# Two banded gated layers on one core: the same instructions in another order within a pipeline step

## Chip, cores and metric

One NeuronCore of a Trainium2 chip runs the whole program. The metric is device time in microseconds (us), from one launch. The engines are TensorE (PE), ScalarE (ACT), VectorE (DVE), GpSimd (POOL) and SyncE (SP), which here only issues DMAs. Each runs its own instruction list in order and waits on semaphores for the others.

## What is computed

The input `x` is one image of 512x512 positions with 64 channels, in float32. Two layers of the same form, with weights of their own, follow each other:

```python
def layer(x):                       # x = x + layer(x), twice
    xn    = ln(group_norm(x)) * norm_scale + norm_bias     # over the 64 channels
    left  = (xn @ Wl + bl) * mask * sigmoid(xn @ Wlg + blg)    # 64 -> 128
    right = (xn @ Wr + br) * mask * sigmoid(xn @ Wrg + brg)
    gate  = sigmoid(xn @ Wog + bog)
    out   = banded(left, right, 4)  # out[i, j] = sum over |d| <= 4 of left[i+d, i] * right[i+d, j]
    out   = (ln(out) * out_norm_scale + out_norm_bias) * gate  # over the 128 channels
    return out @ Wo + bo            # 128 -> 64
```

The band multiplies rows of `right` by a narrow band of `left`, for each of the 128 channels on its own.

## The kernel before

**Tiling.** Rows go in 9 blocks of 64 (a block and its halo). A block is cut into 2 chunks of columns, so a layer has 18 chunks, and a chunk has 16 steps. A step `t` takes one unit: 8 columns of the left half of the image and the same 8 of the right half, 64 rows each, which fill 128 partitions. Layer 1 has 288 steps and a lead-in and run-out, and layer 2 the same. In this text r is `t` modulo 16.

**One loop over steps, written out by hand.** `layer()` is a Python loop over `t`. In each step it calls the helper functions in a fixed order, and `en.*` (class `InOrder`, whose line 373 therefore stands for nearly all instructions in the profile) keeps that order on every engine. Nothing is rescheduled afterwards. So the order of the calls is the order in which each engine, and SP's DMA queue, works. A step works on several units at once, at different stages of a software pipeline:

- `load`, `fetch`, `take_left`, `recall` (SP): DMAs of the unit some steps ahead, of the residual tile `XR` (4 buffers) for step t+1, of band tiles `A`, and of the transposed unit `zg` for step t+2.
- `affine` (POOL, 2 instructions) and `inner_norm` of the unit of step t+2 (POOL, 2 instructions): first normalization, on tile `z`. `inner_stats` (DVE, 4 `BATCH_NORM_STATS2` on `sti`).
- `transposed` of the unit of step t+1 (PE transposes into PSUM), then `kept` (ACT writes `zT`, SP stores it).
- `right` of the unit of step t, in two halves (q = 0 and q = 4): `projected` (PE, from `zT`), a sigmoid (ACT, `sg`), a product (DVE, `RO`).
- `gates` (PE from `zg`, then two ACT sigmoids into `gate`), `turned` (PE transposes of `on`, then two DVE products into `ZH`), `biased` (POOL, adds the bias to `XR`), `end` of step t-1 (PE, from `ZH`; one DVE addition into `XR`; two stores on SP), `sums` of step t-2 (PE, in layer 1 alone), `norm` for step t+1 (ACT, 8 instructions `on<-RO,nm,rs`).
- `mix` (the band, in place on `RO`): 32 matmuls on PE, then one half of the result copied by ACT and one by DVE. DVE's copy waits for ACT's copy of the same band group.
- `out_stats` (DVE, `sto<-RO`), 3 to 7 in a step, called `looking`. `solve`, in steps with r = 0, 4, 8 and 12: five small DVE instructions (`var`, `nm`, `rs`), then twelve small POOL instructions (`rsqrt`, `rs`, `nm`), which give the scales that `inner_norm` (from step t+1 on) and `norm` (called in step t+1) need.

Band groups are not spread evenly, and neither are the POOL affines:

```python
step = [t0 + n for n, k in enumerate((2, 1, 2, 2, 1, 2, 1, 2, 2, 1)) for _ in range(k)]
count = [1, 1, 2, 1, 2, 1, 1, 2, 1, 1, 1, 0, 1, 1, 0, 0]
```

So steps with r = 0, 2, 3, 5, 7, 8 have two band groups, those with r = 1, 4, 6, 9 one, and r = 10 to 15 none. `count` is the number of units that are affined on POOL in a step with that r; in steps with r = 0, 4, 8, 12 the next step's are done as well.

**Buffers that couple the engines.** PSUM pool `ps2` has two buffers, which the right halves, `transposed` and the band groups take in turn. Pool `ps` (3 buffers in layer 1, 4 in layer 2) is taken in turn by the two `gates`, the two `turned` and the `end` of a step. `on` and `gate` have one buffer, `sg` and `zT` two, `ZH` two pairs.

**Short names.** For PE's groups in a step: P0 and P4 are the two halves of the right projection, G the gate matmuls, T the transposes of `turned`, X those of `transposed`, E the matmuls of `end`, S those of `sums`, B one band group. PE's order before is P0, G, P4, T, X, E, S, B, B. ACT's is sigmoid of P0, two gate sigmoids, sigmoid of P4, `zT`, 8 of `norm`, copies. DVE's is up to three `out_stats`, product of P0, up to two `out_stats`, product of P4, the two `ZH` products, other `out_stats`, `inner_stats`, addition of `end`, `solve`, copies.

Of the kernel before, what the change touches and what calls it, by code (L numbers as in the profile page):

```python
# [79 lines left out]
def tile_two_banded_layers(  # L80
# [301 lines left out]
    class Unit:  # L382
# [3 lines left out]

        def __init__(self, at: int, blk: Block = None, j: int = 0, near: int = None):
            self.at, self.blk, self.j, self.near = at, blk, j, near

    def load(src: bass.AP, u: Unit):  # L390
        u.z = zp.tile([P, JU, D], F32, tag="z", name="z")
# [93 lines left out]
        return pr  # L485

    def right(u: Unit, q: int, w: dict):
        pr = projected(u, q, w["right"]).rearrange("p e k h -> p (e k) h")
        sg = wk.tile([P, JQ, H], F32, tag="sg", name="sg", bufs=2)
        en.scalar.activation(sg, pr[:, :, H:], AF.Sigmoid)  # L490
        en.vector.tensor_tensor(
            RO[:, :, u.c + q : u.c + q + JQ, :],
            pr[:, :, :H].rearrange("p j (h t) -> p h j t", t=2),
            sg.rearrange("p j (h t) -> p h j t", t=2), ALU.mult,
        )

    def left(u: Unit, q: int, w: dict):
# [38 lines left out]
            )  # L536
        return A

    def mix(c: int, A: bass.AP, h0: int):


        j0 = c % 2 * (JC - JW)
        R = RO[:, :, j0 : j0 + JC, :]
        pb = two_banks()
        ph = pb.rearrange("i (h j) -> i h j", j=JC)
        for turn in range(2):
            for h in range(HB // 2):
                for e in range(2):
                    part = slice(e * S, (e + 1) * S)
                    hh = (turn ^ e) * (HB // 2) + h  # L550
                    en.tensor.matmul(
                        ph[part, hh, :], lhsT=A[part, :, h0 % HA + hh],
                        rhs=R[part, (h0 + hh) // 2, :, hh % 2],
                        start=True, stop=True,
                    )
        q = HB // 4
        for n in range(2):
            o = R[:, h0 // 2 + n * q : h0 // 2 + (n + 1) * q]
            v = pb.rearrange("i (h t j) -> i h j t", t=2, j=JC)[:, n * q : (n + 1) * q]
            if n == 0:  # L560
                en.scalar.copy(o, v)
            else:
                en.vector.tensor_copy(o, v)

    class Out:

# [40 lines left out]
            for n, o in enumerate(outs):  # L607
                o.rs, o.nm = ro[:, n * JU : (n + 1) * JU], nm[:, n * JU : (n + 1) * JU]

    def norm(o: Out):  # L610
        o.on = onp.tile([P, JU, H], F32, tag="on", name="on")
        for j in range(JU):
            en.scalar.activation(
                o.on[:, j, :].rearrange("p (h t) -> p h t", t=2), RO[:, :, o.c + j, :],
                AF.Identity, bias=o.nm[:, j : j + 1], scale=o.rs[:, j : j + 1],
            )
# [5 lines left out]
    def gates(o: Out, w: dict):  # L622
        b = o.blk
        n = 2 * JQ * b.m
        pgs = [one_bank()[:, :n].rearrange("h (k p) -> h k p", p=b.m) for e in range(2)]
        for e, pg in enumerate(pgs):
            part = slice(e * D, (e + 1) * D)
            en.tensor.matmul(
                pg, lhsT=w["gate"][part],
                rhs=o.t[part].rearrange("c k (e p) -> c (k e) p", e=2)[:, :, b.lo : b.hi],  # L630
                start=True, stop=True,
            )
        g = gp.tile([H, 4 * JQ * (S - WIN)], F32, tag="gate", name="gate")
        for e, pg in enumerate(pgs):
            en.scalar.activation(
                g[:, e * n : (e + 1) * n].rearrange("h (k p) -> h k p", p=b.m), pg, AF.Sigmoid
            )

        o.g = g[:, : 2 * n].rearrange("h (x n p) -> h n x p", n=2, p=b.m)

    def turned(o: Out, w: dict):

        b = o.blk
        pts = [one_bank().rearrange("h (x p) -> h x p", p=S) for n in range(2)]
        for e in range(2):
            for k in range(JQ):
                for n, pt in enumerate(pts):
                    part = slice(n * S, (n + 1) * S)
                    en.tensor.transpose(
                        pt[:, e * JQ + k, :], o.on[part, place(k, e), :], ident[part, part]  # L650
                    )
        for n, pt in enumerate(pts):
            en.vector.scalar_tensor_tensor(
                ZH[(2 * o.n + n) % len(ZH)][:, :, : b.m], pt[:, :, b.lo : b.hi], w["ob"],
                o.g[:, n], ALU.add, ALU.mult,
            )
# [13 lines left out]
        add = fewer if stats and o.blk.m < S - WIN else w["add"]  # L670
        en.gpsimd.tensor_tensor(f, f, mid(add[:n], JU // 2), ALU.add)

    def end(dst: bass.AP, o: Out, w: dict):
        m = o.blk.m
        po = one_bank().rearrange("i (j c) -> i j c", c=D)
        for k in range(JQ):
            for e in range(2):
                for n in range(2):

                    en.tensor.matmul(  # L680
                        po[n * S : (n + 1) * S, 2 * k + e, :],
                        lhsT=ZH[(2 * o.n + n) % len(ZH)][:, e * JQ + k, :], rhs=w["Wo"],
                        start=True, stop=True,
                    )
        f = o.xr[: S + m, :, 1 : 1 + 2 * D]
        en.vector.tensor_tensor(
            f, po[: S + m].rearrange("i (k t) c -> i k (t c)", t=2), f, ALU.add
# [16 lines left out]
    def layer(src: bass.AP, dst: bass.AP, w: dict, stats: bool, then=None):  # L704
# [60 lines left out]
        for t in range(min(loads), last_t + 3):  # L765
# [19 lines left out]
                n = (len(os) - 1) * (JU // 2)  # L785
                looking.append((o, st[:, n : n + JU // 2, :], k))

            for v in looking[:3]:
                out_stats(*v)

            for u in affines.pop(t, []):
                affine(u, en.vector if u.at < NU + 4 else en.gpsimd)
            if t % 4 == 0 and t > NU:
                then_affine = affines.pop(t + 1, [])

            todo = []
            for at, u in inners.get(t, []):
                key = (at + 1) // 4
# [5 lines left out]
                todo += [(u, st[:, n : n + JU // 2, :], k) for k in range(JU // 2)]  # L804
                us.append(u)

            if t in units:
                right(units[t], 0, w)
            for v in looking[3:5]:
                out_stats(*v)  # L810
            if t in outs:
                gates(outs[t], w)
            if t in units:
                right(units[t], JQ, w)
            if t in lefts:
                for q in range(0, min(JU, NEAR * JQ - lefts[t].near), JQ):
                    left(lefts[t], q, w)
            for u in inputs(t + 2):
                inner_norm(u)
            if t in outs:  # L820
                turned(outs[t], w)
            for u in inputs(t + 1):
                transposed(u)
                kept(u)
            if t in outs:
                biased(outs[t], w, stats)
            for v in looking[5:]:
                out_stats(*v)
            for v in todo:
                inner_stats(*v)  # L830
            if t - 1 in outs:
                end(dst, outs[t - 1], w)
            if stats and t - 2 in outs:
                sums(outs[t - 2], t - 2 == first_t, t - 2 == last_t)
            if t % 4 == 0:
                st, us = sti.pop((t + 4) // 4, (None, []))
                so, os = sto or (None, [])
                sto = None
                for u in then_affine:
                    affine(u, en.gpsimd)  # L840
                then_affine = []
                if us or os:
                    solve(w, us, os, st, so)
            if t + 1 in outs:
                norm(outs[t + 1])
            for n, (c, h0) in enumerate(mixes.get(t, [])):
                mix(c, A[c, h0 // HA], h0)

    class Slices:

# [131 lines left out]
```

## Time and profile before

| what | value |
|---|---|
| timed runs | 4960.42, 4958.66, 4958.12 us; median 4958.66 |
| span of the profiled execution | 4957.7 us (its time is not listed apart; the median is 0.96 us above the span) |
| busy share of the span | PE 84%, PE weight loads 71%, DVE 77%, ACT 74%, POOL 77% |
| mean granted TensorE clock | 0.940 |
| first group statistics, before layer 1 | about 300 us, DVE and DMA |
| layer 1, its steps with full work | about 541 to 2436 us from the span's start |
| run-out of layer 1 and lead-in of layer 2 | about 2436 to 2900 us |
| layer 2, its steps with full work | about 2900 to 4680 us |

A line of the profile's groups reads: source line, engine, operation, output tile <- input tiles, shape, xcount, busy time. A timeline line has the start in us from the span's start, the duration, the engine and the group, and in brackets the idle time before it with what ended it. Instructions overlap on an engine, so the pitch (start to start) is shorter than the duration. An idle time that ends with a semaphore from another engine is put down to that engine.

### The profile page before, as it was taken

The page shows a single profiled execution, that of the slowest core. Times are in us where ns is not written, and L with a number is a line of the kernel's source. Part 1 is how long each engine was busy: PE and PEld are TensorE (multiplying, and loading weights), DVE is VectorE, ACT ScalarE, POOL GpSimd, SP SyncE. Part 2 cuts the span into 40 slices and gives each one's busy share as a digit, 9 for nine tenths or more (in the row PEclk, how much of TensorE's full clock was granted, in tenths as well). Part 3 has the DMA queues.
Part 4 walks back from the last instruction along what each step waited for, and adds up shares of the span by engine and source line. Part 5 has one row for each costly group of instructions (what it writes and reads, how often), then busy time and mean ns, then how long its engine had stood idle before and what let it go on. Part 6 is the DMA issues. An engine that isn't in the chain of part 4 may idle for free. (4 is left out here: it accounts for less than half of the span.)

```text
span 4957.7 us, 173298 instructions
## 1 busy us (share of the span) xinstructions
PE 4186.4 (84%) x67090; PEld 3543.6 (71%) x67090; DVE 3836.3 (77%) x9635; ACT 3645.2 (74%) x8156; POOL 3826.5 (77%) x4739
## 2 busy tenths in 40 slices
PE   1036899999999999999974689999999999999998
PEld 0025788888888888888763577777777777777775
DVE  6855788888888888888766578888888888888876
ACT  0013788888888888888872378888888888888888
POOL 0037888888888888888534788888888998889853
PEclk6558999999999999999996899999999999999999
DMA  7844677777777777777653467777777777777765
GB/s 305 338 156 130 182 203 207 204 207 204 204 203 204 205 206 206 202 207 210 187 143 88 129 181 205 202 207 205 203 206 202 205 206 205 208 207 209 209 184 152
DMA packets 905343, 982.32 MB, mean 198 GB/s; under 512 B 114210, under 2 KB 641608, under 8 KB 900168
## 3 DMA queue, kind: packets, MB, share of 16 engines
q1 hardware_dynamic: 899840, 969.73, 66.9%
q8 instruction: 531, 8.70, 0.8%
q14 instruction: 292, 2.39, 0.2%
q10 hardware_dynamic: 4680, 1.50, 0.1%
HBM read 658.42 MB, written 312.46 MB: 196 GB/s over the span
## 5 line engine op out<-in xcount | busy, mean ns | idle before, releaser
L373 ACT ACTIVATE on<-RO,nm,rs 128x128 f32<-128x128 f32 x4608 | 1872.5, 496 | 130.1 <-POOL nm L373 110.3
L373 PE MATMUL banks<-pack,zT 64*128 64x256 f32 x9360 | 1325.0, 405 | 148.6 <-DVE RO L373 67.8
L373 PEld LDWEIGHTS banks<-pack,zT 64*128 64x128 f32 x9360 | 886.7, 194 | 517.6 <-DVE RO L373 220.1
L373 PE MATMUL banks<-RO,A 64*64 64x128 f32 x18432 | 1154.3, 277 | 12.7 <-ACT zT L373 12.7
L373 DVE TENSOR_TENSOR RO<-banks,sg 128x512 f32<-128x512 f32 x1152 | 789.9, 686 | 421.1 <-ACT sg L373 402.9
L373 PEld LDWEIGHTS banks<-RO,A 64*64 64x64 f32 x18432 | 1082.3, 183 | 38.6 <-ACT zT L373 15.2
L373 ACT ACTIVATE sg<-banks 128x512 f32<-128x512 f32 (+1 forms) x1188 | 695.0, 587 | 372.5 <-PE banks L373 288.6
L373 DVE BATCH_NORM_STATS2 sto<-RO 128x6 f32<-128x256 f32 x2304 | 842.8, 413 | 1.2
L373 DVE SCALAR_TENSOR_TENSOR ZH<-bank,pack,gate 128x448 f32<-128x448 f32 (+1 forms) x1152 | 738.4, 683 | 71.5 <-ACT gate L373 46.9
L373 DVE COPY RO<-banks 128x512 f32<-128x512 f32 x576 | 396.3, 691 | 487.6 <-ACT RO L373 487.0
L373 POOL TENSOR_TENSOR z<-z,gb 128x512 f32<-128x512 f32 x536 | 687.1, 1282 | 42.0
L373 PE MATMUL bank<-pack,ZH 128*64 128x64 f32 x18432 | 682.8, 229 | 6.1 <-ACT gate L373 5.6
L373 POOL TENSOR_TENSOR z<-z,ga 128x512 f32<-128x512 f32 x536 | 687.8, 1283 | 0.1
L373 POOL TENSOR_TENSOR z<-z,rs 128x512 f32<-128x512 f32 x586 | 618.0, 1055 | 46.0
L373 PEld LDWEIGHTS bank<-pack,ZH 128*64 128x64 f32 x18432 | 602.1, 141 | 48.2 <-ACT gate L373 9.6
L373 POOL TENSOR_TENSOR z<-z,sti 128x512 f32<-128x512 f32 x586 | 627.2, 1070 | 0.0
L373 ACT ACTIVATE gate<-bank 128x448 f32<-128x448 f32 (+1 forms) x1152 | 565.9, 543 | 81.1 <-PE bank L373 66.9
L373 PEld LDWEIGHTS bank<-ident,on 64*128 64x128 f32 x9216 | 409.7, 140 | 260.5 <-ACT gate L373 145.3
L373 PE MATMUL bank<-ident,on 64*128 64x64 f32 x9216 | 450.2, 227 | 137.9 <-ACT gate L373 107.3
L373 PE MATMUL bank<-zg,pack 64*128 64x448 f32 (+1 forms) x2304 | 559.5, 558 | 2.2 <-DMA zg<-later 1.5
L373 POOL TENSOR_TENSOR XR<-XR,pack 120x512 f32<-120x512 f32 (+1 forms) x352 | 418.4, 1190 | 160.6 <-DMA XR<-in_x_dram 58.9
L373 ACT COPY RO<-banks 128x512 f32<-128x512 f32 x576 | 333.5, 583 | 234.1 <-PE banks L373 234.0
(145 smaller groups left out, 3683.3 us busy)
## 6 DMA issues: line engine op xcount, KB each, us to landing
later<-zT SPq DMA_DIRECT2D x576, 256.0 KB
A<-left_of SPq DMA_DIRECT2D x576, 256.0 KB
zg<-later SPq DMA_DIRECT2D x576, 256.0 KB
z<-in_x_dram SPq DMA_DIRECT2D x576, 128.0 KB
z<-mid_x SPq DMA_DIRECT2D x576, 128.0 KB
gn_x<-in_x_dram SPq DMA_DIRECT2D x16, 4096.0 KB
XR<-in_x_dram SPq DMA_DIRECT2D x448, 112.0 KB
mid_x<-XR SPq DMA_DIRECT2D x448, 112.0 KB
```

Source lines behind the costliest of these rows:

```text
L373: return lambda *a, **k: tc.keep_in_program_order(f(*a, **k))
```

## The change

No instruction is added or removed; the order within a step is another. `right` becomes three calls: projection, sigmoid (`right_gate`), product (`right_end`). `gates`, `turned`, `end` and `mix` each give their second part to a call of its own (`gated`, `times_gate`, `ended`, and the copies in the loop). `norm` is called for instructions 0 to 3 and for 4 to 7. The order after, engine by engine:

- PE: P0, G, P4, T, X, S, E, B, B (`left` first of all, in the few steps that have it).
- ACT: sigmoid of P0, two gate sigmoids, sigmoid of P4, `norm` 0 to 3, `zT`, `norm` 4 to 7, the ACT copies of all band groups.
- DVE: two `out_stats`, product of P0, other `out_stats`, product of P4, `inner_stats`, `solve`, the two `ZH` products, addition of `end`, the DVE copies.
- POOL: `inner_norm`, `affine` (with the next step's), `solve`, `biased`.
- SP: the same order as before.

```diff
     def right(u: Unit, q: int, w: dict):
-        pr = projected(u, q, w["right"]).rearrange("p e k h -> p (e k) h")
-        sg = wk.tile([P, JQ, H], F32, tag="sg", name="sg", bufs=2)
-        en.scalar.activation(sg, pr[:, :, H:], AF.Sigmoid)
+        u.pr[q] = projected(u, q, w["right"]).rearrange("p e k h -> p (e k) h")
+
+    def right_gate(u: Unit, q: int):
+        u.sg[q] = wk.tile([P, JQ, H], F32, tag="sg", name="sg", bufs=2)
+        en.scalar.activation(u.sg[q], u.pr[q][:, :, H:], AF.Sigmoid)
+
+    def right_end(u: Unit, q: int):
         en.vector.tensor_tensor(
...
-    def norm(o: Out):
-        o.on = onp.tile([P, JU, H], F32, tag="on", name="on")
-        for j in range(JU):
+    def norm(o: Out, lo: int, hi: int):
+        if lo == 0:
+            o.on = onp.tile([P, JU, H], F32, tag="on", name="on")
+        for j in range(lo, hi):
...
-            for v in looking[:3]:
-                out_stats(*v)
-
-            for u in affines.pop(t, []):
-                affine(u, en.vector if u.at < NU + 4 else en.gpsimd)
-            if t % 4 == 0 and t > NU:
-                then_affine = affines.pop(t + 1, [])
...
-            if t in units:
-                right(units[t], 0, w)
-            for v in looking[3:5]:
-                out_stats(*v)
-            if t in outs:
-                gates(outs[t], w)
-            if t in units:
-                right(units[t], JQ, w)
             if t in lefts:
                 for q in range(0, min(JU, NEAR * JQ - lefts[t].near), JQ):
                     left(lefts[t], q, w)
+            if t in units:
+                right(units[t], 0, w)
+            if t in outs:
+                gates(outs[t], w)
+            for v in looking[0:2]:
+                out_stats(*v)
+            if t in units:
+                right_gate(units[t], 0)
             for u in inputs(t + 2):
                 inner_norm(u)
+            if t in units:
+                right_end(units[t], 0)
+            if t in outs:
+                gated(outs[t])
+            for u in affines.pop(t, []):
+                affine(u, en.vector if u.at < NU + 4 else en.gpsimd)
+            if t % 4 == 0 and t > NU:
+                then_affine = affines.pop(t + 1, [])
+            if t in units:
+                right(units[t], JQ, w)
+            for v in looking[2:5]:
+                out_stats(*v)
             if t in outs:
                 turned(outs[t], w)
             for u in inputs(t + 1):
                 transposed(u)
-                kept(u)
-            if t in outs:
-                biased(outs[t], w, stats)
+            for u in then_affine:
+                affine(u, en.gpsimd)
+            then_affine = []
+            if stats and t - 2 in outs:
+                sums(outs[t - 2], t - 2 == first_t, t - 2 == last_t)
             for v in looking[5:]:
                 out_stats(*v)
+            if t - 1 in outs:
+                end(outs[t - 1], w)
+            if t in units:
+                right_gate(units[t], JQ)
+            if t + 1 in outs:
+                norm(outs[t + 1], 0, 4)
+            for u in inputs(t + 1):
+                kept(u)
+            if t in units:
+                right_end(units[t], JQ)
             for v in todo:
                 inner_stats(*v)
-            if t - 1 in outs:
-                end(dst, outs[t - 1], w)
-            if stats and t - 2 in outs:
-                sums(outs[t - 2], t - 2 == first_t, t - 2 == last_t)
+            if len(mixing) > 0:
+                c, h0 = mixing[0]
+                mixed.append(mix(c, A[c, h0 // HA], h0))
             if t % 4 == 0:
...
-                for u in then_affine:
-                    affine(u, en.gpsimd)
-                then_affine = []
                 if us or os:
                     solve(w, us, os, st, so)
+            if t in outs:
+                times_gate(outs[t], w)
+            if len(mixing) > 1:
+                c, h0 = mixing[1]
+                mixed.append(mix(c, A[c, h0 // HA], h0))
             if t + 1 in outs:
-                norm(outs[t + 1])
-            for n, (c, h0) in enumerate(mixes.get(t, [])):
-                mix(c, A[c, h0 // HA], h0)
+                norm(outs[t + 1], 4, 8)
+            if len(mixing) > 0:
+                en.scalar.copy(*mixed[0][0])
+            if len(mixing) > 1:
+                en.scalar.copy(*mixed[1][0])
+            if t - 1 in outs:
+                ended(dst, outs[t - 1])
+            if len(mixing) > 0:
+                en.vector.tensor_copy(*mixed[0][1])
+            if t in outs:
+                biased(outs[t], w, stats)
+            if len(mixing) > 1:
+                en.vector.tensor_copy(*mixed[1][1])
```

## Prediction

> **What bounds the kernel now.** I read first the page's shares, then the engines' busy time in the stretch of each layer with full work, then single steps in the timeline, then the waits of layer 2.
>
> ```profile
> PE 4186.4 (84%) x67090; PEld 3543.6 (71%) x67090; DVE 3836.3 (77%) x9635; ACT 3645.2 (74%) x8156; POOL 3826.5 (77%) x4739
> ```
> ```profile
> 541.00:2436.00 1895.00, 1817.18 (x31539) 1588.30 (x31539) 1537.18 (x3856) 1590.72 (x3550) 1667.30 (x2019) 0.99 0.72 204
> 2899.60:4680.00 1780.40, 1636.20 (x25892) 1385.19 (x25888) 1466.48 (x3655) 1503.10 (x3354) 1591.43 (x1917) 0.99 0.72 205
> ```
> Four engines are busy for over 80% of the full stretches (columns PE, PEld, DVE, ACT, POOL), so a reordering can only win stalls. One step of layer 1 with one band group, on PE:
>
> ```profile
> 1263.67 1.14 PE L373 MATMUL banks<-pack,zT 64*128 64x256 f32 x8
> 1264.64 0.92 PE L373 MATMUL bank<-zg,pack 64*128 64x448 f32 x4
> 1265.39 1.03 PE L373 MATMUL banks<-pack,zT 64*128 64x256 f32 x8
> 1266.26 0.69 PE L373 MATMUL bank<-ident,on 64*128 64x64 f32 x16
> 1266.81 0.46 PE L373 MATMUL banks<-ident,z 64*128 64x64 f32 x8
> 1267.20 1.15 PE L373 MATMUL bank<-pack,ZH 128*64 128x64 f32 x32
> 1268.18 0.64 PE L373 MATMUL acc<-XR 120*64 120x65 f32 x16
> 1268.75 2.11 PE L373 MATMUL banks<-RO,A 64*64 64x128 f32 x32
> 1270.79 1.13 PE L373 MATMUL banks<-pack,zT 64*128 64x256 f32 x8
> ```
> PE never waits: pitches P0 0.97, G 0.75, P4 0.87, T 0.55, X 0.39, E 0.98, S 0.57, B 2.04, sum 7.12. Two bands make 8.95. Layer 2 has no S: 6.53 and 8.53. A step without a band is ACT's:
>
> ```profile
> 3703.37 0.58 ACT L373 ACTIVATE sg<-banks 128x512 f32<-128x512 f32 x1
> 3703.85 0.95 ACT L373 ACTIVATE gate<-bank 128x448 f32<-128x448 f32 x2
> 3704.70 0.59 ACT L373 ACTIVATE sg<-banks 128x512 f32<-128x512 f32 x1
> 3705.32 0.60 ACT L373 ACTIVATE zT<-banks 128x512 f32<-128x512 f32 x1
> 3705.82 3.23 ACT L373 ACTIVATE on<-RO,nm,rs 128x128 f32<-128x128 f32 x8
> 3708.94 0.59 ACT L373 ACTIVATE sg<-banks 128x512 f32<-128x512 f32 x1
> ```
> No gap, 5.57 a step, while PE needs 4.50. From gate sigmoid to gate sigmoid, the steps r = 0 to 15 of one chunk take 8.9, 7.1, 9.0, 9.0, 7.1, 9.6, 7.0, 9.0, 9.0, 7.0, 5.9, 5.7, 5.7, 7.5, 5.7, 5.7 in layer 1 and 8.4, 6.5, 9.2, 8.5, 6.5, 11.1, 6.5, 9.2, 8.8, 6.5, 6.4, 5.6, 5.6, 7.7, 5.9, 5.7 in layer 2. Over 16 full chunks of each the mean is 119.3 and 118.7. The stalls to win are what exceeds the pitches: r = 5 and 13, and in layer 2 r = 2, 7 and 10. Two are `solve`'s:
>
> ```profile
> 3714.79 0.29 POOL L373 TENSOR_TENSOR rsqrt<-rs 128x64 f32<-128x64 f32 x1 [0.67 <-DVE rs L373]
> 3719.40 3.22 ACT L373 ACTIVATE on<-RO,nm,rs 128x128 f32<-128x128 f32 x8 [1.87 <-POOL nm L373]
> 3659.79 3.33 ACT L373 ACTIVATE on<-RO,nm,rs 128x128 f32<-128x128 f32 x8 [1.28 <-POOL nm L373]
> 3664.37 1.13 PE L373 MATMUL banks<-pack,zT 64*128 64x256 f32 x8 [1.54 <-DVE RO L373]
> ```
> POOL's part of `solve` takes 4.61 (3714.79 to 3719.40); `norm` waits for it, at r = 13 and 5, and at r = 5 the band copies behind `norm` hold P0 of the next step.
>
> **The change, part by part.** Its instructions stay; each term is a stall, per chunk. A step starts at P0 = 0.
>
> *Steps without a band.* G starts at 0.97, the gate sigmoid 1.00 later (a step above: 1264.64, and ACT at 1265.64), the sigmoid of P4 0.89 after that, `norm` 0 to 3 at 3.36, `zT` 4x0.39 later at 4.93, and P0 of the next step 0.65 after `zT` starts (the bound pairs of `zT` and P0 show 0.64 to 0.65): a ring of 5.58. ACT's own work is 5.57. So 5.6 for 5.69 in layer 1 and 5.57 in layer 2: -0.4 and +0.1 over the steps other than r = 10 and 13. The sums of DVE (5.43 with five `out_stats`) and PE lie inside it.
>
> *r = 13.* At r = 12 DVE runs product of P0 at 2.04, four `out_stats` of 0.33, product of P4, `solve`: `rs` at 5.3 from P0. POOL comes there at about 5.3 too, since `biased` (1.15) now stands behind `solve`. `norm` may start 4.61 later plus 0.07, at 9.98; due is 5.6+3.36 = 8.96. The wait is 1.0, the step 6.6: -1.0 in layer 1, -1.1 in layer 2. `zT` is now queued behind this wait, and P0 behind `zT`.
>
> *r = 5.* In layer 1 POOL comes earlier by `biased` and `nm` is ready at 1298.9, before it is due (P0 1295.88+3.36): the step falls to PE's 8.95, -0.65. In layer 2 POOL is the later one: `nm` at about 3658.3 against 3656.6 due, then 1.57+0.50+1.57 to the ACT copy, 0.6 to DVE's, 0.75 to P0, 3663.3 instead of 3664.37: -1.1.
>
> *Behind steps with one band, layer 2 (r = 2, 7, 10).* DVE's copy comes 0.2 earlier (ACT's copy at 7.03 from P0, before 7.22), and two `out_stats` instead of three stand ahead of the product that X waits for (0.33): -0.45 at r = 2 and 7, -0.7 at r = 10, where the step returns to 5.75. Layer 1 at r = 10: -0.25.
>
> *r = 0, layer 2.* Seven `out_stats` of which five stand ahead of the product of P4, which the first band's buffer waits for: +0.3. Layer 1 has S as cover.
>
> *`solve` on DVE while POOL works.* Here is a row against the change: in layer 2 one small `var` on DVE took 1.14 instead of 0.18, beside a POOL `z<-z,gb` of 1.47 (usual 1.28). Before, POOL mostly idles when DVE solves; after, it often still affines.
>
> ```profile
> 3653.36 1.47 POOL L373 TENSOR_TENSOR z<-z,gb 128x512 f32<-128x512 f32 x1
> 3653.72 1.14 DVE L373 TENSOR_SCALAR var<-var 128x32 f32<-128x32 f32 x1
> ```
> One blocked instruction (0.96) delays the `ZH` products, the addition and the copies now queued behind `solve`: hidden at r = 12, 0 at r = 0, +0.6 at r = 4, +1.0 at r = 8. I take half, +0.8, in layer 2 and +0.2 in layer 1; bounds 0 and +1.6.
>
> [...]
>
> *Free.* S before E: both are ready, PE's sum is the same. `biased` last on POOL: the addition that needs it comes a step later, with 0.5 to 1 us left behind r = 4 and 12. SP: the addition ends where it did (6.1 to 7.5 from P0), so stores, loads and fetches behind it keep their place; if that slips, POOL waits for `XR`. Lead-in: `left` is ahead of `right`, so the 10 us wait of `sg` for its store moves from the next step into its own; 5 such steps a layer, 0 taken, bounds -10 and +10 in all.
>
> Sum: layer 1 -1.0-0.65-0.4-0.25+0.2 = -2.1; layer 2 -1.1-1.1-0.9-0.7+0.3+0.8+0.1-0.1 (r = 14) = -2.7. Times 16 chunks: -34-43 = -77. The profiled span of 4957.7 lies 0.96 below the median of 4958.66; I predict 4882. Bounds per chunk: all stalls gone and no new one, -3.3 and -6.0, gives 4810; none gone and the new ones full, +0.8 and +2.5, gives 5011.
>
> **Rivals.**
> *Slower: the ring holds the steps without a band.* ACT works in order; `norm` 0 to 3 and its waits (for T, for `nm`) now stand ahead of `zT`, so PE no longer runs ahead of ACT: before, P0 started 3.1 ahead of its gate sigmoid in these steps, in the ring it is 1.97. Each 0.1 of latency that I missed costs 0.1x6x32 = 19. From 0.4 a step it eats the whole gain; with 0.5 and r = 13 as late as before (+32) the time is 4882+96+32 = 5010. For it: the ring has 0.01 of room. Against: every latency in it is read from a bound pair.
>
> *Less: POOL sets layer 2.* Its pitches in a chunk (`inner_norm`, `affine`, `biased`, `solve`, from the timeline) are 16x(2.14+2.60+1.15)+4x4.53 = 112.3, and its waits for `rs` stay:
>
> ```profile
> POOL rsqrt L373 <- DVE rs L373: 89.7, 60, 3.6
> ```
> 5.6 a chunk. If they don't shrink, layer 2 gains 1 a chunk: 4958.7-34-16 = 4909.
>
> *More: the waits for `rs` vanish.* Both layers fall towards POOL's 112.3 and PE's 112.7 in layer 1 (16x5.08+6x3.87+4x2.04), say 114.5: -(4.8+4.2)x16 = -144, 4815.
>
> *Nothing:* the stalls only change their names, 4959.
>
> **How the numbers follow.** Forecast (4840 to 4895) 0.42, less gain 0.17, more gain 0.10, no change 0.05, slower 0.26. I call 0.2%, about 10 us, what a measurement of this kernel can tell. Faster is 0.69, same 0.05, slower 0.26. The range of 8 in 10 runs from 4805 to 4990: it leaves out about half of the largest gains and half of the slower case.
>
> **What would show it.** Right: steps r = 10 to 12 near 5.6 and 13 near 6.6 in both layers, r = 5 at 8.95 and about 10.0, `on` waiting for `nm` near 1.0 at r = 13, DVE's wait for ACT's copy (168 in layer 2) mostly filled. [...]

## The result, and the profile after

The changed kernel takes 4875.28 us (median of 4 runs, 4872.71 to 4880.72), the kernel before 4959.54 beside it (4 runs, 4958.12 to 4965.5): a ratio of 0.9831, interval 0.9817 to 0.9845. The span of the profiled execution is 4874.6, 83.1 less than before.

The page's first lines and two of its groups (busy time, mean ns | idle time ahead, and who ended it):

```profile
PE 4107.5 (84%) x67090; PEld 3507.8 (72%) x67090; DVE 3830.6 (79%) x9635; ACT 3642.8 (75%) x8156; POOL 3804.8 (78%) x4739
...
L373 ACT ACTIVATE on<-RO,nm,rs 128x128 f32<-128x128 f32 x4608 | 1924.3, 492 | 68.3 <-POOL nm L373 53.7
L373 PE MATMUL banks<-pack,zT 64*128 64x256 f32 x9360 | 1335.1, 407 | 358.1 <-ACT zT L373 281.3
```

The busy times of ScalarE, VectorE and GpSimd moved by 22 us at most; what went is mainly stalls. PE's busy time fell by 79 us, 75 of them in the two full stretches, for a reason that was not taken apart. The granted clock's means of 0.940 before and 0.97 after differ mostly by the first 300 us (0.54 and 1.00), where PE is busy for 21 and 23 us. `norm` waits for `nm` half as long as before (53.7 us, before 110.3), while PE's projections now wait for `zT` 281.3 us, before 64.8. Busy time per engine in the two full stretches (16 chunks each):

```profile
558.40:2417.80 1859.40, 1794.69 (x31729) 1584.85 (x31725) 1546.37 (x3876) 1611.01 (x3583) 1668.79 (x2024) 1.00 0.74 209
2873.40:4728.30 1854.90, 1706.61 (x27645) 1459.11 (x27642) 1565.94 (x3876) 1596.30 (x3584) 1669.59 (x2024) 0.99 0.74 210
```

The span falls into six stretches, cut at gate sigmoids (first r = 0 step, the one 16 chunks later, the last gate of the layer):

| us | before | after | change | forecast |
|---|---|---|---|---|
| start to the first r = 0 of layer 1 | 541.0 | 558.4 | +17.4 | 0 |
| 16 chunks of layer 1 | 1909.4 | 1859.4 | -50.0 | -34 |
| rest of layer 1, to its last gate | 173.8 | 162.8 | -11.0 | 0 |
| from there to the first r = 0 of layer 2 | 275.4 | 292.8 | +17.4 | 0 |
| 16 chunks of layer 2 | 1899.7 | 1854.9 | -44.8 | -43 |
| rest, to the end | 158.4 | 146.3 | -12.1 | 0 |

The sum forecast was near the truth, but partly by terms that cancel: both lead-ins got longer, which the working took as 0, and both run-outs shorter, which it did not have. The steps, from gate sigmoid to gate sigmoid, as medians over the chunks:

| r | L1 before | L1 after | forecast | L2 before | L2 after | forecast |
|---|---|---|---|---|---|---|
| 0 | 8.87 | 8.88 | | 8.48 | 8.87 | 8.8 |
| 1, 4, 6 | 7.0 to 7.1 | 7.03 | 7.1 | 6.54 | 6.54 | 6.5 |
| 2, 7 | 9.0 | 8.87 | 9.0 | 9.17 | 8.57 | 8.7 |
| 3 / 8 | 8.97 / 8.96 | 8.87 | 9.0 | 8.53 / 8.83 | 8.37 / 8.98 | 8.5 / 8.8 |
| 5 | 9.61 | 8.88 | 8.95 | 11.09 | 10.05 | 10.0 |
| 10 | 5.95 | 5.59 | 5.7 | 6.43 | 5.80 | 5.75 |
| 11, 12 | 5.7 | 5.6 | 5.6 | 5.6 | 5.57 | 5.6 |
| 13 | 7.56 | 6.74 | 6.6 | 7.73 | **8.55** | 6.6 |
| 14 | 5.72 | 5.59 | 5.6 | 5.89 | 5.61 | 5.8 |

A step without a band, in the timeline of ACT after the change, in the order foretold:

```profile
3656.45 0.98 ACT L373 ACTIVATE gate<-bank 128x448 f32<-128x448 f32 x2
3657.34 0.60 ACT L373 ACTIVATE sg<-banks 128x512 f32<-128x512 f32 x1
3657.85 1.69 ACT L373 ACTIVATE on<-RO,nm,rs 128x128 f32<-128x128 f32 x4
3659.44 0.57 ACT L373 ACTIVATE zT<-banks 128x512 f32<-128x512 f32 x1
3659.92 1.66 ACT L373 ACTIVATE on<-RO,nm,rs 128x128 f32<-128x128 f32 x4
```

No idle time stands between them. The one step that went wrong is r = 13 of layer 2, here from the timelines of PE (P0 of the step r = 12 before it), POOL and DVE (its `solve`), then ACT and PE:

```profile
3660.07 1.14 PE L373 MATMUL banks<-pack,zT 64*128 64x256 f32 x8 [1.01 <-ACT zT L373]
...
3663.99 1.27 POOL L373 TENSOR_TENSOR z<-z,gb 128x512 f32<-128x512 f32 x1
3664.60 0.70 DVE L373 TENSOR_SCALAR var<-sti 128x32 f32<-128x32 f32 x1
...
3665.93 0.29 POOL L373 TENSOR_TENSOR rsqrt<-rs 128x64 f32<-128x64 f32 x1 [0.67 <-DVE rs L373]
...
3670.53 1.68 ACT L373 ACTIVATE on<-RO,nm,rs 128x128 f32<-128x128 f32 x4 [1.44 <-POOL nm L373]
3672.11 0.57 ACT L373 ACTIVATE zT<-banks 128x512 f32<-128x512 f32 x1
...
3672.73 1.73 PE L373 MATMUL banks<-pack,zT 64*128 64x256 f32 x8 [2.16 <-ACT zT L373]
3674.24 1.71 PE L373 MATMUL bank<-zg,pack 64*128 64x448 f32 x4
```

`norm` waits 1.44 for `nm`, `zT` is queued behind it, PE idles 2.16 us, and then P0 lasts 1.73 instead of 1.13 and G 1.71 instead of 0.92. The granted clock (third column from the right) in the two stretches around it:

```profile
3669.20:3672.60 3.40, 1.38 (x40) 1.17 (x38) 3.40 (x10) 2.07 (x6) 3.16 (x6) 1.00 0.65 175
3672.60:3676.00 3.40, 3.27 (x14) 2.21 (x16) 1.31 (x4) 2.23 (x6) 3.24 (x5) 0.58 0.57 175
```

In the first PE is busy for 1.38 of 3.40; in the second the clock falls to a mean of 0.58. The full stretch of layer 2 has such a fall behind 12 of its 16 passes of r = 13; two of those without it take 7.09 and 6.85, where the others take 7.65 to 8.85.

Such falls were not new. The kernel before has ten in its full stretch of layer 2 and six in that of layer 1, all in the step after, r = 14, which then takes 5.8 to 7.15 us instead of 5.6 in layer 2 and 6.3 to 6.45 instead of 5.7 in layer 1. The clock stands at half for 51.2 and 20.5 us there, after the change for 44.4 and 0. The medians of the table hide this; one of the ten, in the kernel before:

```profile
3723.40:3730.20 6.80, 6.23 (x54) 4.86 (x56) 5.36 (x13) 5.42 (x14) 6.64 (x7) 0.50 0.50 148
```

### The profile page after: what moved, and what is told of

It reads as the page before. It is cut to its first block, busy times and chain, and to the rows that moved or that the text cites. A ratio compares the mean times of both kernels' runs of the same rounds, so it can differ in the third digit from the quotient of the medians.

```text
span 4874.6 us, 173394 instructions
## 1 busy us (share of the span) xinstructions
PE 4107.5 (84%) x67090; PEld 3507.8 (72%) x67090; DVE 3830.6 (79%) x9635; ACT 3642.8 (75%) x8156; POOL 3804.8 (78%) x4739
## 3 DMA queue, kind: packets, MB, share of 16 engines
q10 hardware_dynamic: 4680, 1.50, 0.1%
## 4 chain that ended last, share of the span: by engine, by line
PE 56%; DVE 15%; ACT 12%; POOL 6%; DMA 4%; issue 3%; SPq 3%; ACTq 0%; POOLq 0%; DVEq 0%
PE banks L373 36%; PE bank L373 18%; ACT on L373 6%; DVE gn_st L373 3%; POOL rsqrt L373 3%; DVE RO L373 3%; SPq L373 3%; PE acc L373 3%; DVE sto L373 3%; ACT gate L373 2%; ACT zT L373 2%; DVE sti L373 2%; DVE ZH L373 2%; ACT sg L373 1%; DVE var L373 1%
## 5 line engine op out<-in xcount | busy, mean ns | idle before, releaser
L373 ACT ACTIVATE on<-RO,nm,rs 128x128 f32<-128x128 f32 x4608 | 1924.3, 492 | 68.3 <-POOL nm L373 53.7
L373 PE MATMUL banks<-pack,zT 64*128 64x256 f32 x9360 | 1335.1, 407 | 358.1 <-ACT zT L373 281.3
L373 PE MATMUL bank<-pack,ZH 128*64 128x64 f32 x18432 | 651.4, 224 | 4.7 <-ACT gate L373 4.3
L373 PEld LDWEIGHTS bank<-pack,ZH 128*64 128x64 f32 x18432 | 587.2, 138 | 26.3 <-ACT gate L373 7.9
L373 DVE BATCH_NORM_STATS2 sti<-z 128x6 f32<-128x128 f32 x2344 | 504.2, 282 | 12.9 <-POOL z L373 12.7
```

The costliest lines, as they stand in the source:

```text
L373: return lambda *a, **k: tc.keep_in_program_order(f(*a, **k))
```

## The experiments

All were compared with runs of the kernel before in the same group (medians 4956.5 to 4959.6) and are read against the changed kernel's 4875.28 unless said otherwise. Diffs are against the changed kernel.

**1. `left` behind P4's product**

```diff
-            if t in lefts: ... left(lefts[t], q, w)     # first of the step
...
             if t in units:
                 right_end(units[t], JQ)
+            if t in lefts: ... left(lefts[t], q, w)
```

> The changed kernel with the call of left moved from the head of the step to behind the product of P4; nothing else differs. Theory (left's place costs the lead-in): in the changed kernel the first gate of layer 1 came at 544.4 us instead of 529.3, and the lead-in of layer 2 took 279.6 instead of 263.8. With left behind P4 both go back: first gate near 530, lead-in of layer 2 near 264, and the time falls by about 31 to 4844 (4836 to 4852); the full steps keep their lengths. Rival (another part of the new order delays the lead-in, such as the DVE or POOL order): first gate stays at 544 and the time within 5 us of 4875.

Measured: 4877.19, ratio to before 0.9838 (0.9824 to 0.9853). Both lead-ins stay 17 us too long (+17.4 and +16.8). The place at the head of the step is not, by itself, what costs. The wait of `sg` for the store moved to the next step, as in the kernel before, and still took up to 14.6 us, where it took up to 10.6 before.

**2. E twice at r = 13 of layer 2**

```diff
-                end(outs[t - 1], w)
+                end(outs[t - 1], w, 1 + (not stats and t % NU == 13))
```

> The changed kernel, with the 32 matmuls E issued twice (same operands, same result) at r = 13 of layer 2 alone, about 1.0 us more work for PE in a place where it idles 2.16 us before P0. Theory (the granted clock): the idle time of PE behind the wait for nm makes the granted clock 0.5 in the next stretch, which is about 1.5 of the step's 8.55 us; with the idle time cut to about 1.2 (layer 1 has 1.47 and no such stretch) the stretches of half clock vanish, r = 13 falls to about 7.0, its mean from 8.08 to 7.0, and the time by about 17 to 4858 (4850 to 4864). Rival (the step is long because of the wait for nm and what follows it, and the clock has no part): r = 13 stays at 8.0 to 8.6 and the time within 4 us of 4875, or rises by up to 16 if the added matmuls delay P0.

Measured: 4854.95, 0.9792 (0.9777 to 0.9806): more work, and 20 us less time. The mean of r = 13 goes from 8.08 to 7.10, and no fall of the clock is left in the full stretch of layer 2. P0 behind that step in the timeline of PE, and the stretch that follows P0:

```profile
3660.79 1.13 PE L373 MATMUL banks<-pack,zT 64*128 64x256 f32 x8 [1.24 <-ACT zT L373]
```
```profile
3660.50:3663.90 3.40, 3.11 (x38) 2.52 (x40) 1.60 (x4) 3.40 (x9) 3.32 (x4) 1.00 0.51 163
```

P0 is back at 1.13 and the clock at 1.00. The clock theory holds: of the excess of r = 13 in layer 2, about 1.0 a chunk in the mean is the clock, and r = 14 loses another 0.2 with it (5.79 to 5.58).

**3. `solve` ahead of the next step's affines on POOL**

```diff
-            for u in then_affine:
-                affine(u, en.gpsimd)
-            then_affine = []
...
                     solve(w, us, os, st, so)
+            for u in then_affine:
+                affine(u, en.gpsimd)
+            then_affine = []
```

> The changed kernel with the affines of the next step (two POOL instructions of 1.28 us a unit) moved from ahead of solve to behind it in the steps with r = 0, 4, 8, 12. Theory (DVE's var and POOL's affine hold each other up, and nm comes late by it): var falls from 0.70 to 0.85 (1.22 at r = 4) to about 0.18 in all solves, POOL waits for rs instead of the other way round, the wait of on for nm at r = 13 falls from 1.44 to about 0.9 in layer 2 and from 0.86 to about 0.2 in layer 1; r = 13 becomes 6.6 (8.08 in the mean) in layer 2 and 6.1 (6.74) in layer 1, r = 5 in layer 2 about 9.3 (10.05): in all about -2.2 and -0.6 a chunk, -45 us, 4830 (4820 to 4845). Rival (the wait is POOL's sum of work, only moved): the affined unit is late for its statistics in the next step, inner_stats waits for z at r = 1, 5, 9 and 13, and the time stays within 8 us of 4875 or rises.

Measured: 4874.94, 0.9831 (0.9817 to 0.9846): nothing, the rival's time, though not by its wait. `var` at r = 12 of layer 2 still takes 0.70 and `norm` still waits 1.45 (medians). In layer 2 POOL runs from one `solve` to the next almost without a gap (its only waits there are 68.0 us for `rs`), so the unit moved behind one `solve` is in front of the next, and POOL comes at the same time as it did. The experiment therefore did not free `var` and says nothing on its price.

**4. `zT` ahead of an undivided `norm`**

```diff
-            if t + 1 in outs:
-                norm(outs[t + 1], 0, 4)
             for u in inputs(t + 1):
                 kept(u)
+            if t + 1 in outs:
+                norm(outs[t + 1], 0, 4)
```

> The changed kernel with zT ahead of norm 0 to 3 on ACT, so that the eight instructions of norm follow each other; nothing else differs. Theory (the queue on ACT: at r = 13 zT, and with it P0 of the next step, waits behind the wait for nm): PE no longer idles 2.16 us there, no stretch of half clock follows, r = 13 of layer 2 falls from 8.55 (mean 8.08) to about 7.0, that of layer 1 keeps its 6.7, and the steps without a band stay at 5.6, since ACT's own sum of 5.57 sets them and PE runs ahead again: -17 us, 4858. Rival (the split is what makes the ring work): zT waits for X, which ends at about 3.5 us from P0 while the sigmoid of P4 ends at 3.4, ACT loses 0.1 to 0.3 in every step, the steps without a band rise to 5.7 to 5.9, and the time goes up by 20 to 60 us.

Measured: 4839.27, 0.9762 (0.9746 to 0.9778), 36 us better than the change. r = 13 falls to 6.30 in layer 2 and, unexpectedly, to 6.01 in layer 1; no fall of the clock is left in the full stretch of layer 2. The timeline of ACT at r = 13 of layer 2:

```profile
3641.38 0.60 ACT L373 ACTIVATE zT<-banks 128x512 f32<-128x512 f32 x1 [0.26 <-PE banks L373]
3642.39 3.24 ACT L373 ACTIVATE on<-RO,nm,rs 128x128 f32<-128x128 f32 x8 [0.42 <-POOL nm L373]
```

`zT` passes ahead of the wait, and the wait itself is 0.42. The rival had a part: layer 1's steps without a band are 5.69 instead of 5.59, and layer 2's r = 2 and 7 are 8.91 instead of 8.57. So the split is worth a tenth where nothing waits, and costs more where `nm` is late. It shortens both lead-ins by 5 to 6 as well.

**5. `left` between P4 and X, with the old order in its steps**

```diff
             if t in units:
                 right(units[t], JQ, w)
+            if t in lefts:
+                right_gate(units[t], JQ)
+                right_end(units[t], JQ)
+                for q in ...: left(lefts[t], q, w)     # and not at the other places
```

> The changed kernel, but in the few steps that compute left (all in the lead-ins) every call stands as in the kernel before: P0, P4, their sigmoids and products, then left, and only then T, X, zT and the rest. All other steps are as changed. Theory (sg has two buffers, and left fills both: the next sigmoid of right waits until left's store has landed, about 10 us; left ahead of the sigmoids puts the whole wait into the step, left behind X and zT puts it into the next one, and only left between P4 and X lets X, zT and SP's store of zT pass in it): the lead-in of layer 1 shortens by about 15 (first gate near 529), that of layer 2 from 279.6 to about 264, and the time falls by 30 to 4846 (4838 to 4854). Rival (the 15 us come from a part of the new order that has nothing to do with left): within 6 us of 4875.

Measured: 4861.25, 0.9804 (0.9787 to 0.982). The lead-ins go from +17.4 and +17.4 to +7.9 and +9.3. Half of the theory: the calls around `left` make about half of the loss. The waits of ACT in the lead-in of layer 2, of the changed kernel and then of this one:

```profile
ACT sg L373 <- DMA left_of<-sg: 52.8, 4, 14.9
```
```profile
ACT sg L373 <- DMA left_of<-sg: 39.3, 4, 14.0
```

**6. `biased` ahead of `solve` on POOL**

```diff
+            if t in outs:
+                biased(outs[t], w, stats)
             for u in then_affine:
...
-            if t in outs:
-                biased(outs[t], w, stats)
             if len(mixing) > 1:
```

> The changed kernel with biased (one POOL instruction of 1.18 us) back ahead of the next step's affines and of solve. Theory (POOL's arrival at solve sets nm, and nm sets r = 13 and r = 5): r = 13 of both layers gets longer by 0.9 to 1.2, to about 7.8 in layer 1 and 9.4 in layer 2 (the stretch of half clock stays), r = 5 by 0.3 to 0.6 in layer 1 and 0.8 to 1.1 in layer 2, in all about 1.5 and 2 a chunk, +56 us, 4931 (4905 to 4945). Rival (DVE's rs sets nm, and biased is free on POOL): within 10 us of 4875.

Measured: 4918.22, 0.9919 (0.9905 to 0.9934): +43 against the change, within the theory's range. r = 12 and 13 of layer 1 together get 1.07 longer in the mean, r = 5 is longer by 0.29 and 0.33. At r = 12 and 13 of layer 2 only 0.2 appears, and r = 13 gets shorter (7.54) where the theory had 9.4: the stall is now shared by two steps, and 5 falls of the clock follow instead of 12. r = 4 of layer 2, which the theory did not name, is longer by 0.33 in the mean.

**7. `zT` first only at r = 1, 5, 9, 13**

```diff
+            if t % 4 == 1:
+                for u in inputs(t + 1):
+                    kept(u)
             if t + 1 in outs:
                 norm(outs[t + 1], 0, 4)
-            for u in inputs(t + 1):
-                kept(u)
+            if t % 4 != 1:
+                for u in inputs(t + 1):
+                    kept(u)
```

> The changed kernel with zT ahead of norm 0 to 3 on ACT only in the steps with r = 1, 5, 9 and 13, where norm waits for the nm of the solve in the step before; in the other steps zT stays behind norm 0 to 3. Theory (zT behind the wait for nm is what the split costs, and in steps without that wait the split is worth 0.1 to 0.3 a step): r = 13 falls to 6.0 in layer 1 and 6.3 in layer 2 and r = 5 of layer 2 to 9.6, as with zT always first, while the steps r = 10 to 12 keep 5.6 and r = 2 and 7 of layer 2 their 8.57: about -0.7 and -2.4 a chunk against the changed kernel, 4827 (4818 to 4835). Rival (the two parts don't add: with PE ahead of ACT behind r = 13 and 5, the later steps lose again what the split gave, as POOL or DVE is next): no better than the 4839 of the kernel with zT first in every step.

Measured: 4850.3, 0.9782 (0.9767 to 0.9796): better than the change, but the rival holds against experiment 4. Layer 1 gains from both parts (115.73 a chunk, 116.21 changed, 115.94 in experiment 4), though less than the 0.7 foretold. In layer 2 r = 8 takes 9.31 instead of the 8.96 of experiment 4 and r = 14, in the mean, 6.20 instead of 5.58, seven falls of the clock follow r = 13 there, and the chunk is 115.02 against 114.61.

**8. Three `out_stats` ahead of the product of P0**

```diff
-            for v in looking[0:2]:
+            for v in looking[0:3]:
...
-            for v in looking[2:5]:
+            for v in looking[3:5]:
```

> The changed kernel with three out_stats instead of two ahead of the product of P0 on DVE (and two instead of three ahead of that of P4). Theory (X waits for that product, which frees its PSUM buffer): in layer 2 the steps r = 2, 7 and 10, behind band copies, get longer by up to 0.33 each, and the steps with band groups of layer 1, whose T-to-X distance fell by 0.06 with the change, by 0.06 to 0.1 each; together +1.0 and +0.6 a chunk, +25 us, 4900 (4885 to 4908). Rival (DVE has slack there, and the shorter steps come from S ahead of E or the later copies): within 5 us of 4875.

Measured: 4875.85, 0.9832 (0.9817 to 0.9847). The total is the rival's, the mechanism in part the theory's: r = 10 of layer 2 does not move (5.81). In layer 1 the steps r = 1 to 8 are about 0.09 longer each, +8.3 us over the stretch. In layer 2 r = 2 and 7 are 0.15 and 0.25 longer, but r = 0 falls back from 8.87 to 8.54 and r = 5 from 10.05 to 9.73, and the stretch is 6.0 shorter.

**9. `solve` behind the `ZH` products and the addition on DVE**

```diff
-            if t % 4 == 0:  ... solve(w, us, os, st, so)     # ahead of times_gate
             if t in outs:
                 times_gate(outs[t], w)
...
                 ended(dst, outs[t - 1])
+            if t % 4 == 0:  ... solve(w, us, os, st, so)
```

> The changed kernel with solve back behind the two ZH products and the addition of end on DVE, as in the kernel before; the copies stay last. Theory (solve's place on DVE makes rs, nm and with them r = 13 and r = 5 early; this is the largest part of the gain): rs comes 1.9 later (two pitches of 0.59 and one of 0.60, plus waits for T's banks), r = 13 gets longer by 1.3 to 1.9 in both layers, r = 5 by 0.3 to 0.6 in layer 1 and 0.7 to 1.5 in layer 2: about +2 a chunk in each layer, +65 us, 4940 (4915 to 4965). Rival (in layer 2 POOL, not DVE, comes last to solve, and in layer 1 ACT has slack at r = 13): under +25, 4875 to 4900, and the gain came from elsewhere.

Measured: 5049.68, 1.0191 (1.0174 to 1.0208): +174, far over the theory's 65 and even slower than the kernel before. The page's row for `norm`, now idle for `nm` three times as long:

```profile
L373 ACT ACTIVATE on<-RO,nm,rs 128x128 f32<-128x128 f32 x4608 | 1926.1, 493 | 217.8 <-POOL nm L373 155.5
```

r = 13 is 9.77 and 9.86 and r = 5 10.45 and 11.78: both late in both layers, and with `zT` behind `norm` each late `nm` holds PE (its projections wait 392.1 us for `zT`, changed 281.3). The clock falls in 15 of the 16 passes of each layer, where the changed kernel has 0 and 12, so a part of the 174 is the clock's; how much was not taken apart. Both run-outs return to the lengths of before (+0.3 and +0.1).

**10. The same place of `solve` alone, on the kernel before** (this diff is against the kernel before)

```diff
                     solve(w, us, os, st, so)
+            if t in outs:
+                times_gate(outs[t], w)      # the two ZH products, taken out of turned
+            if t - 1 in outs:
+                ended(dst, outs[t - 1])     # the addition and its stores, taken out of end
```

> The kernel before with one part of the change alone: on DVE the two ZH products and the addition of end stand behind solve instead of ahead of it. PE, ACT, POOL and the rest of DVE keep the old order (zT ahead of an undivided norm, biased ahead of solve, left between P4 and X). Theory (solve's place on DVE is the main part of the gain, and alone worth about as much as the whole change, since the split of norm and left's place cost what biased gains): POOL waited 116 us, 1.8 a solve, for rs in layer 1 and 0.7 to 1.9 a solve in layer 2, so r = 13 falls by 1.0 to 1.3 and r = 5 to 8.95 in layer 1, and in layer 2 both by about 0.65; about -1.9 and -1.3 a chunk, and the two run-outs shorten by 11 and 12 as in the change: 4959 - 30 - 21 - 23 = 4885 (4870 to 4900). Rival (biased ahead of solve makes POOL the last to come, so that an earlier rs is only waited out): a gain under 30, 4930 or more.

Measured: 4883.87, 0.9847 (0.9831 to 0.9864), the theory's 4885. One part alone brings 76 of the change's 84 us: -15.4 and -32.8 in the full stretches, -14.4 and -11.0 in the run-outs, and the lead-ins keep their length. The total meets the theory better than its parts do, which were -30, -21 and -23: r = 13 falls to 6.57 and 6.98 and r = 5 to 9.23 and 10.10, but r = 12 of layer 1 grows from 5.68 to 6.25. In the full stretches the clock falls 3 times instead of the 16 of the kernel before, and r = 14, where those falls were, is about 13 of the 76 us. The edit also puts the `ZH` products behind the other `out_stats` and `inner_stats` in every step; r = 1 to 3 and 9 to 11 keep their lengths within 0.01, so this shows no gain of its own there. The page's row for `norm`:

```profile
L373 ACT ACTIVATE on<-RO,nm,rs 128x128 f32<-128x128 f32 x4608 | 1870.2, 495 | 25.0 <-POOL nm L373 11.3
```

**11. `left` into a buffer of its own**

```diff
-        sg = wk.tile([P, JQ, H], F32, tag="sg", name="sg", bufs=2)     # in left
+        if q == 0:
+            u.sl = onp.tile([P, JU, H], F32, tag="on", name="on")
+        sg = u.sl[:, q : q + JQ, :]
```

> The changed kernel, left still at the head of its steps, but its sigmoids write into the tile of on, which nothing else uses in the lead-ins, instead of the two buffers of sg. Theory (the lead-ins' waits are the sg buffers', held until left's store has landed): the 103.2 us in which ACT's sg waited for left_of<-sg vanish; of about 13 us in each of the eight waits some three quarters are on the path, the two lead-ins shorten by 30 to 50 each, and the time falls to 4800 (4785 to 4830). Rival (the stores themselves are the limit, whatever buffer they read): the wait moves to zT's store, to the next left or to DVE and SP, and the gain stays under 20: 4855 to 4878.

Measured: 4857.95, 0.98 (0.9785 to 0.9814). All waits of `sg` for `left`'s store are gone, yet the lead-ins win only 9.6 and 11.8 of the 17.4. In layer 2's lead-in ACT now waits instead for the store of `zT`, a wait that the changed kernel's list did not have (that of the kernel before had 18.6 us of it):

```profile
ACT zT L373 <- DMA later<-zT: 28.8, 5, 7.8
```

So the rival's time came true. A part of the wait only moved to another store; that the stores are the limit whatever buffer they read is not shown beyond that.

**12. What the runs point to, together**: `zT` first in all steps of layer 2 and at r = 1, 5, 9, 13 of layer 1, experiment 5's `left`, and three `out_stats` first at r = 0 of layer 2.

```diff
+            ahead_of = 3 if not stats and t % NU == 0 else 2
...                                                   # experiment 5's part
+            first = not stats or t % 4 == 1
+            if first:
+                for u in inputs(t + 1): kept(u)
             if t + 1 in outs:
                 norm(outs[t + 1], 0, 4)
...
+            if not first:
+                for u in inputs(t + 1): kept(u)
```

> The changed kernel with what the runs so far point to, put together: zT ahead of norm 0 to 3 in all steps of layer 2 and in the steps with r = 1, 5, 9, 13 of layer 1; left between P4 and X with the old order in its steps; three out_stats ahead of the product of P0 at r = 0 of layer 2. If the parts add: 4839 (zT first) - 3 (the split kept in layer 1's other steps) - 15 (left) - 5 (r = 0) = 4816 (4808 to 4826). If they don't, as in the mixed order of zT: 4830 to 4840.

Measured: 4828.55 (4 runs, 4823.45 to 4833.01), 0.9742 (0.9727 to 0.9756): faster than both kernels, 130 us under the kernel before beside it (4958.82). It is between the two expectations. The lead-ins gained (6.8 and 6.9 over before); against experiment 4, r = 0 of layer 2 gained its 0.3 (8.63 for 8.94) and r = 5 gave it back (9.94 for 9.60).

## Why the prediction was right, and where not

**Steps without a band: right.** 5.59 in layer 1 against 5.58 worked out, 5.57 in layer 2. The slower rival, that the ring loses time in every step, fell. The latencies of its bound pairs were the right ones to add up.

**r = 5, 2, 7, 10 and 0: right** within 0.15 (table above). Experiment 8 shows the reason given for r = 0 and for r = 2 and 7: put the third `out_stats` back and r = 0 loses its +0.3 while r = 2 and 7 lose part of their gain. At r = 10 the number came true and that reason did not: experiment 8 leaves it at 5.81. Undoing the split (experiment 4) takes back 0.35 at r = 2 and 7 and 0.28 at r = 10, more than the 0.2 that the working gave to the earlier copy.

**r = 13, layer 2: wrong.** The forecast step was 6.6, from a wait of 1.0 for `nm`. It is 8.55, with a wait of 1.44 (layer 1 came near, with 6.74 and 0.86). Two steps of the working failed. First, "One blocked instruction (0.96) delays the `ZH` products, the addition and the copies now queued behind `solve`: hidden at r = 12" looked at DVE's queue alone. P0 of the step shown was at 3660.07. POOL ended its affine 5.19 later (3663.99 + 1.27), close to the 5.3 foretold, but DVE's `var`, begun at 4.53, ended only with it: `rs` came late, POOL waited 0.67, and began at 5.86. The 0.5 is the difference between the two waits, 1.44 and 1.0. Second, and larger, "`zT` is now queued behind this wait, and P0 behind `zT`" stood there with no price. Its price was idle time of PE that cost the clock: about 1.0 a chunk (experiment 2), and the whole of the queueing about 36 us (experiment 4), 11 of them in the lead-ins.

In the trace the 12 passes of r = 13 in layer 2 with a fall of the clock behind them have idle gaps of PE of 2.14 to 2.16 us, and the passes in layer 1, with gaps of at most 1.47, have no fall.

**Layer 2's sum: -45 for -43 by luck.** In means, r = 13 grew by 0.18 a chunk where -1.1 was forecast. The 1.3 were made up by terms that missed the other way: the +0.8 for `solve` on DVE came to 0.1 (r = 4 and 8), r = 2 and 7 gave 0.2 more than forecast, r = 14 0.3 more, and r = 3 and 15 another 0.26. The working took layer 2's two-band step for PE's sum at 8.53; its own pitches give 5.08 - 0.57 + 3.87 = 8.38, and r = 3 fell to 8.37. What r = 14 gave goes with the clock, whose falls stood at r = 14 and now stand at r = 13.

**`solve` on DVE while POOL works: there, but its term was too large.** The working had +0.6 at r = 4 and +1.0 at r = 8 and took half. r = 4 kept its 6.54, and r = 8 went from 8.83 to 8.98. The median of `var<-sti` in layer 2 went from 0.177 to 0.325; the groups of `var` in layer 2's full stretch, before and then after (ns, min/median/max):

```profile
L373 DVE TENSOR_SCALAR var<-sti x63: 159/177/1259, 2879.0 to 4720.7; 128x32 f32<-128x32 f32 x63
```
```profile
L373 DVE TENSOR_SCALAR var<-sti x64: 158/325/756, 2876.3 to 4709.0; 128x32 f32<-128x32 f32 x63, 128x8 f32<-128x8 f32 x1
```

Of the 64 `solve`s of that stretch after the change, 24 have none of the five DVE instructions above 0.29 us, 27 have one, and 13, all at r = 4, have two (medians 0.38 for `var<-sti` and 1.22 for `var<-var`), none more: one, as taken, is too few at r = 4. That POOL's instruction holds them is read from their common end, within 0.05 us in all 53 cases. What it costs in time stays open beyond the 0.5 worked out above: experiment 3 was meant to remove it and did not.

**Layer 1: the gain was undersized**, -50 for -34. Steps with bands were taken as unchanged at PE's sum. r = 1 to 4, 7 and 8 fell by 0.09 to 0.14, since the distance from T to X was partly a wait for the product of P0, behind three `out_stats`. Experiment 8 returns 0.09 a step of it. These steps make about 10 us of the 16. Another 5.6 are r = 14 (5.95 to 5.60 in the mean): the six falls of the clock there are gone, a gain that the working did not have.

**The lead-ins: the term "0 taken, bounds -10 and +10" failed.** They cost +17.4 each. The text had named the wait of `sg` for `left`'s store, and moved it without pricing what stands behind it. Experiment 5 gives half to the calls around `left`; the split of `norm` has 5 or 6 (experiment 4). The rest was not taken apart.

**The run-outs were not in the sum at all**: -11.0 and -12.1. They have fewer steps with full work but the same `solve`s; experiment 9 takes the gain away to within 0.3, experiment 10 brings it alone.

**Which part carried it.** The working spread the gain over five terms. By experiments 9 and 10 the place of `solve` on DVE carries nearly all, a part of it through the clock, and by 6 `biased` behind it carries 43 in the new order. The split of `norm` (-36 when undone) and the lead-ins work against it. The effects don't add: undoing `solve`'s place costs 174 in the new order, where `zT` waits behind `norm`, and it gives 76 alone in the old one, where `zT` doesn't. That this difference makes the gap between 174 and 76 fits PE's longer wait for `zT` in experiment 9, but no run shows it by itself.

The rival "POOL sets layer 2" was near without deciding. POOL waited this long for `rs` in its full stretch after the change:

```profile
POOL rsqrt L373 <- DVE rs L373: 61.9, 62, 6.2
```

That is over 15.6 chunks (2874 to 4680 us), 4.0 a chunk; the 89.7 of before were over 15.0, 6.0 a chunk. The rival let them stand, at 5.6, since it divided by 16 chunks; they shrank by 2.0, and layer 2 gained 2.8.

One sign named beforehand failed besides the wait at r = 13: DVE's wait for ACT's copy in layer 2, 167.9 us before, was not mostly filled. In the same stretch of 15.6 chunks:

```profile
DVE RO L373 <- ACT RO L373: 147.3, 205, 1.2
```

## What to carry to other kernels

An instruction that may wait for a late producer must not stand ahead of one that another engine needs at once: the same four instructions of `norm` ahead of `zT` were worth 0.1 us in layer 1's steps without that wait, and at r = 13, with it, cost 0.7 us in layer 1 and 1.8 in layer 2 (mean, the clock's part included). Move the few small instructions of a long cross-engine chain (here five of DVE, 0.6 us in all where nothing holds them up) ahead of the large ones first, and measure that move alone; here it brought 76 of 84 us. Price the lead-in and run-out as stretches of their own, since there the order met other limits than in the steady steps (+17.4 us for each lead-in, -11.0 and -12.1 for the run-outs).

## What was not expected of the hardware

More work on TensorE made the program faster: a gap of 2.16 us was followed by 3.4 us at half the granted clock, and 1.0 us of repeated matmuls in that gap took 20 us off the program. Gaps of 1.24 (experiment 2) and up to 1.47 us (layer 1) at the same step had no such effect. In layer 2 the 12 passes of the changed kernel with gaps of 2.14 to 2.16 us had it, and the other four had not, of which three have gaps of 2.08 to 2.15 and one has 1.39. So the length of the gap does not decide alone. What else decides is not shown here: no run moved a gap in time and changed nothing else.
